# A fused graph-network kernel: two layer-1 steps a turn in the last gate blocks, adjacencies two packs ahead, head rounds with conv1 first

## The chip, the cores and the metric

The kernel runs on one core of one Trainium2 chip. The metric is the device time of the program in microseconds. Before the change it is 2128.19 us, the median of three runs (2126.38 to 2130.4). Engines are named as in the profile: PE (TensorE matmuls) and PEld (its weight loads), DVE (VectorE), ACT (ScalarE), POOL (GpSimd) and SP (SyncE, which here only issues DMAs). Line numbers are those of the kernel before.

## The reference, cut to what matters

Two residual layers over `x` of 128 graphs x 128 nodes x 256 features, all in float32.

```python
# layer 0
h = relu(layernorm(x))
hc = relu(bn1(conv1(h^T)))                    # 1x1 convolution over features
x_conv = relu(bn2(conv2(hc)) + h^T)^T         # 17 taps along the nodes
A = exp(-dist(h @ w_se)) * adj                # 128x128 per graph
x_nmp = A @ relu(h @ w_msg + b_msg)
x = x + GRU([x_conv, x_nmp], h)               # gates r, z, n
# layer 1: only nodes 0 to 24, in 5 groups of 25, 9, 7, 6 and 6 nodes
h = relu(layernorm(x))
for g in range(5):
    a = sym_norm(adj[g] + I)                  # degree^-1/2 on both sides
    fused[nodes of g] += w[g] * relu(a @ (relu(a @ (h_g @ W1[g]) + b1[g]) @ W2[g]) + b2[g])
x = x + fused
```

Rows of nodes 25 and up are final after layer 0 (up to the residual); layer 1 needs layer 0 of its graphs complete.

## The kernel before

A block is four graphs (512 node rows, `BB = 4`), so there are 32 blocks, in two halves of 16. The program has three stages.

**Heads and spectra.** conv2 is done as a product of spectra. Each half runs `heads` (L249): for block i the layer norm (`head_norm`, DVE with a power on POOL, L144 to L151), the transposes to features-first (`head_turn`, PE L201, ACT L202, stored to DRAM at L203), conv1 (`head_conv1`, PE L215, DVE L218, ACT L219) and the block's spectra (`head_spectra`, PE L230, copied into `X` by DVE L236 and ACT L238). The pieces of different blocks are staggered within one round of the loop. Beside the first half the spectra of the taps are made, `weight_spectra` (L165): 8 groups of 4 steps, 32 in all; a step is 16 matmuls into four PSUM banks (L172), emptied by two DVE (L178) and two ACT (L180) copies, and after its fourth step a group of 2,560 KB goes to DRAM (L182). `some_spectra(k)` takes k steps; six are taken ahead of `heads`, and `heads` calls it at its two `between()` places a round. Then `spectral` (L266) multiplies the spectra, 40 frequencies a half, with `v` loaded from DRAM; it begins the next half's heads near its end (`heads_begin`).

**Gates.** For each of 32 blocks `gates` (L530) computes the three GRU gates by a seven-product scheme; each unit has seven products (PE L550), and after each product it calls `between()`, 22 times a block with the one at L588. That is `step` (L845): odd calls advance `beside_gates(i + 1)` (messages, inverse transform, edges and the residual `back(i - 1)` for other blocks), and even calls, and odd ones once that is exhausted, take one step of layer 1. `back` (L608) transposes the first 25 nodes (PE L622, waiting for DVE's L617) and stores them to DRAM as rows `xg`.

**Layer 1.** The graphs are cut into parts of 32, 32, 32, 16, 8 and 8 (`PARTS`). `layer1(k)` (L690) is a generator that starts when all blocks of part k are through; part 4 starts behind block 30, part 5 in the tail. A part's graphs are packed by group into up to 128 rows. For a pack: `pack_load` (L645: `adj`, `hg` from DRAM), `pack_rows` (L655: degree and norm, DVE with a power on POOL L670, and a block-diagonal matrix `bd`, L676 and L679), `pack_adj` (L682: PE transposes `bd`, L685, and DVE scales it into `nt`, L687). Then a step is one pack's first product with `nt` (PE L766, DVE L767), or W1 of half the hidden columns of a group in this chunk (PE L783, ACT/DVE L788/L790), or W2 of one pack (PE L800, ACT L802) with the closing product of the pack before (`last`, PE L729, ACT L732, DVE L738). `prepare(j)` runs these stages ahead: loads of pack j + 5, rows of j + 3, `nt` of j + 1. A part waits 8 empty steps after its first loads. W1 and W2 of a group are loaded into rings of 2 and 3 buffers (L704), and a part's result is stored at L813.

The order on each engine is fixed when the program is built: a list scheduler moves instructions within what the dependences and the rings of buffers allow, and an engine then runs its list in order. DMAs issued on SP run through one such list as well, so a DMA that waits holds up those listed behind it. The tail is written out by hand: finish all but the last generator, run part 4 until it says that all its packs are loaded, start part 5, finish.

Of the kernel before, what the change touches and what calls it, by code (L numbers as in the profile page):

```python
# [66 lines left out]
def gnn_kernel(ctx: ExitStack, tc: tile.TileContext, io, out0: bass.AP, out1: bass.AP):  # L67
# [119 lines left out]
    def head_load(wk, i, queue):  # L187
        xs[i] = wk.tile([P, BB, D], F32, tag="ln", name="ln", bufs=3)
        queue.dma_start(xs[i], x[i * BB:(i + 1) * BB].rearrange("b n d -> n b d"))
# [4 lines left out]
    def head_turn(wk, i):  # L194

        ln = xs.pop(i)
        ht = wk.tile([P, C, T], F32, tag="ht", name="ht", bufs=2)
        for c in range(C):
            ps = bank()
            for b in range(BB):  # L200
                nc.tensor.transpose(ps[:, b * N:(b + 1) * N], ln[:, b, c * P:(c + 1) * P], ident)  # L201
            nc.scalar.activation(ht[:, c, :], ps, AF.Relu)  # L202
        nc.scalar.dma_start(htd[i], ht)  # L203
        hcs[i] = ht
# [44 lines left out]
    def heads(wk, X, h, between):  # L249

        i0, i1 = h * NBH, (h + 1) * NBH
        for i in range(i0, i1 + 1):
            if i + 3 < i1:
                head_load(wk, i + 3, nc.sync)
            if i + 2 < i1:
                head_norm(wk, i + 2)
            if i + 1 < i1:
                head_turn(wk, i + 1)
            between()
            if i < i1:  # L260
                head_conv1(wk, i)
            between()
            if i > i0:
                head_spectra(X, i - 1)
# [60 lines left out]
    with front as es:  # L325
        xp = es.enter_context(tc.tile_pool(name="xp", bufs=1))
        hk = es.enter_context(tc.tile_pool(name="hk", bufs=1))
        X = xp.tile([P, C, NP_, 2, P], F32)
        with ExitStack() as ws:
            wp = ws.enter_context(tc.tile_pool(name="wp", bufs=1))  # L330
            todo = [(c, q) for c in range(C) for q in range(D // WCH)]
            head_load(hk, 0, nc.scalar)
            nc.sync.dma_start(gt, io["gt"])
            taps = [taps_load(wp, *todo[k]) for k in range(2)]
            head_norm(hk, 0)
            spectra = []

            def some_spectra(k=1):
                for _ in range(k):
                    if not spectra and todo:  # L340
                        spectra.append(weight_spectra(wp, *todo.pop(0), taps.pop(0)))
                    if spectra and next(spectra[0], STOP) is STOP:
                        spectra.pop(0)
                        if len(todo) > 1:
                            taps.append(taps_load(wp, *todo[1]))
                        some_spectra()

            some_spectra(3)
            constants()
            heads_begin(hk, 0)  # L350
            some_spectra(3)
            heads(hk, X, 0, some_spectra)
            while spectra or todo:
                some_spectra()
        bp = es.enter_context(tc.tile_pool(name="bp", bufs=1))
        nc.sync.dma_start(wms, io["wms"].rearrange("(c p) o -> p c o", p=P))
        nc.sync.dma_start(bms, row("bms", D + 3))
        nc.sync.dma_start(fw, row("fw", 5))
        nc.sync.dma_start(wih, io["wih"].rearrange("(c p) o -> p c o", p=P))
        nc.sync.dma_start(whh, io["whh"].rearrange("(c p) o -> p c o", p=P))  # L360
        for h in range(NH):
            if h:
                heads(hk, X, h, lambda: None)
            spectral(bp, X, h, lambda: heads_begin(hk, h + 1) if h + 1 < NH else None)
            if h == 0:
                gate_weights()
# [278 lines left out]
    def pack_load(k, g, b0, nb):  # L645
        s = GROUPS[g][0]
        n = nb * s
        adj = l1.tile([P, NN], F32, tag="adj", name="adj", bufs=6)
        r0 = (first_of[k] + b0) * s
        nc.sync.dma_start(adj[:n, :s], io[f"adj{g}"][r0:r0 + n, :])  # L650
        hg = l1.tile([P, D], F32, tag="hg", name="hg", bufs=6)
        nc.sync.dma_start(hg[:n], xg[k][g][b0 * s:b0 * s + n, :])
        return adj, hg

# [35 lines left out]
    def layer1(k):  # L690
# [20 lines left out]

        def prepare(j):

            if 0 <= j + 5 < len(packs):
                loads[j + 5] = pack_load(k, *packs[j + 5])
            if 0 <= j + 3 < len(packs):
                g, _, nb = packs[j + 3]
                rows[j + 3] = pack_rows(g, nb, *loads.pop(j + 3))
            if 0 <= j + 1 < len(packs):
                g, _, nb = packs[j + 1]  # L720
                ready[j + 1] = pack_adj(nb * GROUPS[g][0], *rows.pop(j + 1))

        def last(g, b0, nb, s2, nt):

# [13 lines left out]
                    nc.vector.tensor_add(fv, fv, ov[:, c, :, at:at + rn])  # L738
                at += rn

        for j in (-5, -4):
            prepare(j)
        part_rows(k)
        nc.sync.dma_start(f[:, :, :size, :], xf[k])
        yield
        weights1(2)
        weights2(3)
        for _ in range(8):
            yield
        for j in (-3, -2, -1):  # L750
            prepare(j)
            yield
        ends = {g: n + 1 for n, (g, _, _) in enumerate(packs)}
        j = 0
        for chunk in chunks:
# [3 lines left out]
            for g, b0, nb in chunk:  # L759
                n = nb * GROUPS[g][0]  # L760
                prepare(j)
                hg, nt = ready.pop(j)
                j += 1
                ps = bank()
                for c in range(C):
                    nc.tensor.matmul(ps[:, c * P:c * P + n], hg[:n, c * P:(c + 1) * P], nt[:n, :n], start=True, stop=True)  # L766
                nc.vector.tensor_copy(ax[:, :, at:at + n], ps[:, :C * P].rearrange("p (c m) -> p c m", c=C)[:, :, :n])  # L767
                work.append((g, b0, nb, nt, at))
                segs[g] = (segs[g][0] if g in segs else at, at + n)
                at += n  # L770
                if late:
                    last(*late.pop(0))
                yield j + 5 >= len(packs)
            hh = l1.tile([P, HID // P, 512], F32, tag="hh", name="hh", bufs=1)
            for g, (m0, m1) in segs.items():
                m = m1 - m0
# [64 lines left out]
    for i in range(NBLK):  # L841
        first = beside_gates(i + 1)
        turn = [0]

        def step():  # L845

            turn[0] += 1
            if turn[0] % 2 and next(first, STOP) is not STOP:
                return
            while layer1s and next(layer1s[0], STOP) is STOP:  # L850
                layer1s.pop(0)

        if i + 2 < NBLK:
            load(i + 2)
        xts[i] = wk.tile([P, C, T], F32, tag="xt", name="xt", bufs=2)
        nc.sync.dma_start(xts[i], io["xT"][i])

        def nxt():
            for _ in first:
                pass  # L860
            if i + 1 < NBLK:
                gate_inputs(i + 1)

        gates(i, step, nxt)
        for k in range(len(PARTS)):
            if i * BB == first_of[k + 1]:
                layer1s.append(layer1(k))
# [106 lines left out]
```

## Time and profile before

The span of the profiled execution is 2127.4 us. By stages, from the busy time of each engine in windows:

| stage, us from the start | length | PE busy | DVE busy | PE clock | DMA share |
|---|---|---|---|---|---|
| setup, 0 to 28.9 | 28.9 | 17.9 | 19.9 | 0.84 | 0.93 |
| heads, first half, to 204.0 | 175.1 | 159.3 | 109.6 | 0.90 | 0.70 |
| spectral, first half, to 318.6 | 114.6 | 107.4 | 56.8 | 0.97 | 0.79 |
| heads, second half, to 430.7 | 112.1 | 105.3 | 73.9 | 0.97 | 0.45 |
| spectral, second half, to 535.0 | 104.3 | 103.1 | 50.0 | 1.00 | 0.81 |
| gates with layer 1, to 1949.0 | 1414.0 | 1390.5 | 914.7 | 0.99 | 0.29 |
| blocks 30 (its end) and 31, to 2018.6 | 69.6 | 58.2 | 43.6 | 0.93 | 0.19 |
| rest of part 3, to 2033.4 | 14.8 | 14.7 | 2.6 | 0.85 | 0.75 |
| part 4, to 2076.5 | 43.1 | 36.7 | 18.9 | 0.76 | 0.52 |
| part 5, to 2127.4 | 50.9 | 40.4 | 12.9 | 0.71 | 0.22 |

"PE clock" is the share of full speed that was granted. A matmul in float32 shows up as two records, so 16 records of L215 are 8 instructions. The granted clock matters as much as busy time here: a busy PE at clock 0.7 does 0.7 of the work.

### The profile page before, as it was taken

The page shows a single profiled execution, that of the slowest core. Times are in us where ns is not written, and L with a number is a line of the kernel's source. Part 1 is how long each engine was busy: PE and PEld are TensorE (multiplying, and loading weights), DVE is VectorE, ACT ScalarE, POOL GpSimd, SP SyncE. Part 2 cuts the span into 40 slices and gives each one's busy share as a digit, 9 for nine tenths or more (in the row PEclk, how much of TensorE's full clock was granted, in tenths as well). Part 3 has the DMA queues.
Part 4 walks back from the last instruction along what each step waited for, and adds up shares of the span by engine and source line. Part 5 has one row for each costly group of instructions (what it writes and reads, how often), then busy time and mean ns, then how long its engine had stood idle before and what let it go on. Part 6 is the DMA issues. An engine that isn't in the chain of part 4 may idle for free.

```text
span 2127.4 us, 30421 instructions
## 1 busy us (share of the span) xinstructions
PE 2033.4 (96%) x10725; PEld 1696.2 (80%) x10725; DVE 1302.8 (61%) x3576; ACT 712.9 (34%) x1456; POOL 574.7 (27%) x666
## 2 busy tenths in 40 slices
PE   7888998999899999999999999999999999998988
PEld 6777888988687887877888787788878878886776
DVE  6665456645366676676666567666666766657532
ACT  3333113411233333333333333333333333332322
POOL 3101441144142342432222243222223322222100
PEclk8989999999999999999999999999999999999977
DMA  8665885378622222322233232223323222322152
GB/s 335 251 229 207 283 277 192 130 234 281 190 66 70 73 72 80 95 68 59 79 90 103 79 101 66 60 74 94 99 77 99 64 64 77 98 66 73 55 167 77
DMA packets 209689, 263.34 MB, mean 124 GB/s; under 512 B 60290, under 2 KB 182146, under 8 KB 204802
## 3 DMA queue, kind: packets, MB, share of 16 engines
q1 hardware_dynamic: 201202, 223.12, 34.6%
q10 hardware_dynamic: 8336, 38.28, 4.9%
q8 instruction: 86, 1.41, 0.3%
q14 instruction: 65, 0.53, 0.1%
HBM read 179.30 MB, written 85.72 MB: 125 GB/s over the span
## 4 chain that ended last, share of the span: by engine, by line
PE 83%; DVE 5%; DMA 2%; POOL 1%; issue 1%; SPq 0%; ACT 0%; POOLq 0%; DVEq 0%; ACTq 0%
PE bank L550 35%; PE bank L299 6%; PE bank L800 5%; PE bank L783 5%; PE bank L586 5%; PE bank L456 5%; PE bank L215 3%; PE bank L294 3%; PE bank L441 3%; PE bank L502 3%; PE bank L439 3%; PE bank L230 2%; PE bank L766 1%; PE bank L489 1%; PE bank L729 1%
## 5 line engine op out<-in xcount | busy, mean ns | idle before, releaser
L550 PE MATMUL bank<-t,sw 128*128 128x256 f32 x1024 | 253.6, 380 | 0.0
L563 POOL TENSOR_TENSOR u<-u,m 128x256 f32<-128x256 f32 x96 | 71.7, 747 | 641.5 <-ACT m L561 618.5
L550 PEld LDWEIGHTS bank<-t,sw 128*128 128x128 f32 x1024 | 187.6, 191 | 23.3 <-issue 1.1
L550 PE MATMUL bank<-t,wih 128*128 128x256 f32 x768 | 197.2, 379 | 0.0
L550 PEld LDWEIGHTS bank<-t,wih 128*128 128x128 f32 x768 | 145.5, 190 | 33.8 <-issue 10.0
L291 POOL TENSOR_TENSOR vs<-v 128x512 f32<-128x512 f32 x78 | 101.4, 1319 | 140.3 <-DMA v<-vd 89.1
L783 PE MATMUL bank<-ax,w 128*128 128x192 f32 (+12 forms) x592 | 130.8, 373 | 5.4 <-DMA w<-in_w_dram 3.9
L800 PE MATMUL bank<-w,hh 128*100 128x256 f32 (+8 forms) x552 | 134.6, 389 | 0.0
L215 PE MATMUL bank<-wc,ht 128*128 128x256 f32 x512 | 129.7, 411 | 1.6 <-DVE sp L178 1.6
L456 PE MATMUL bank<-wms,ht 128*128 128x259 f32 x512 | 126.0, 390 | 4.7 <-DMA ht<-htd 4.7
L783 PEld LDWEIGHTS bank<-ax,w 128*128 128x128 f32 x592 | 106.5, 222 | 23.1 <-issue 13.4
L670 POOL TENSOR_TENSOR pw<-pw,mhalf 100x2 f32<-100x2 f32 (+7 forms) x69 | 51.2, 743 | 260.6 <-DVE pw L666 92.7
L215 PEld LDWEIGHTS bank<-wc,ht 128*128 128x128 f32 x512 | 103.9, 208 | 18.1 <-DVE sp L178 1.8
L456 PEld LDWEIGHTS bank<-wms,ht 128*128 128x128 f32 x512 | 99.9, 195 | 21.0 <-issue 5.1
L550 PE MATMUL bank<-xc,wih 128*128 128x256 f32 x384 | 115.8, 383 | 0.0
L550 PE MATMUL bank<-xn,wih 128*128 128x256 f32 x384 | 115.6, 383 | 0.0
L586 PE MATMUL bank<-ht,whh 128*128 128x512 f32 x256 | 115.2, 592 | 0.0
L738 DVE TENSOR_TENSOR f<-f,og 128x48 f32<-128x48 f32 (+7 forms) x192 | 56.4, 326 | 95.7 <-ACT og L732 94.2
L800 PEld LDWEIGHTS bank<-w,hh 128*100 128x100 f32 (+8 forms) x552 | 92.9, 170 | 27.2
L289 DVE SCALAR_TENSOR_TENSOR s<-X 128x256 f32<-128x256 f32 x78 | 51.7, 665 | 90.6 <-PE bank L299 90.3
L149 POOL TENSOR_TENSOR rs<-ve,mhalf 128x4 f32<-128x4 f32 x32 | 32.3, 1010 | 239.1 <-DVE ve L147 239.1
L460 ACT ACTIVATE msg<-msg 128x512 f32<-128x512 f32 x64 | 40.3, 630 | 157.6 <-DVE msg L457 145.3
(173 smaller groups left out, 4457.0 us busy)
## 6 DMA issues: line engine op xcount, KB each, us to landing
v<-vd SPq DMA_DIRECT2D x80, 512.0 KB
w<-in_w_dram SPq DMA_DIRECT2D x60, 512.0 KB
vd<-sp SPq DMA_DIRECT2D x8, 2560.0 KB
yd<-ys ACTq DMA_DIRECT2D x40, 512.0 KB
htd<-ht ACTq DMA_DIRECT2D x32, 512.0 KB
ht<-htd SPq DMA_DIRECT2D x32, 512.0 KB
ym<-yd SPq DMA_DIRECT2D x32, 512.0 KB
xt<-in_xT_dram SPq DMA_DIRECT2D x32, 512.0 KB
```

What stands on the lines that cost most here:

```text
L215: nc.tensor.matmul(pv[:, bb, :], ht[:, c, b * N:(b + 1) * N], wc1[:, c, :], start=c == 0, stop=c == C - 1)
L291: nc.gpsimd.tensor_tensor(vs, vr, vi, op=ALU.add)
L294: nc.tensor.matmul(p1[:, :D], a[:, c], vs[:, c], start=c == 0, stop=c == C - 1)
L299: nc.tensor.matmul(ps[:, k * D:(k + 1) * D], u[:, c], w[:, c], start=c == 0, stop=c == C - 1)
L439: nc.tensor.matmul(ps, yr[:, o * P:(o + 1) * P], idr, start=True, stop=False)
L441: nc.tensor.matmul(ps[:, b * N:(b + 1) * N], ym[:, b, o * P:(o + 1) * P], idm, start=False, stop=b == BB - 1)
L456: nc.tensor.matmul(ps[:, :D + 3], ht[:, c, b * N:(b + 1) * N], wms[:, c, :], start=c == 0, stop=c == C - 1)
L550: nc.tensor.matmul(ps, w, d, start=n == 0, stop=n == len(pairs) - 1)
L563: nc.gpsimd.tensor_tensor(got["u4"], got["u2"], got["m5"], op=ALU.add)
L586: nc.tensor.matmul(ps, whh[:, c, col:col + P], ht[:, c, :], start=c == 0, stop=c == C - 1)
L783: nc.tensor.matmul(pv[:, q - q0, :], w1s[g][:, c, q * P:(q + 1) * P], ax[:, c, m0:m1], start=c == 0, stop=c == C - 1)
L800: nc.tensor.matmul(ps[:n, :D], hh[:, q, at:at + n], w2s[g][:, q, :], start=q == 0, stop=q == HID // P - 1)
```

## The change

Four edits. In `heads` a round's order becomes conv1(i), tap steps, turn(i+1), norm(i+2), tap steps, spectra(i-1), in both halves; and in the first half each `between()` takes two tap steps instead of one, so that the taps are through by block eight. In layer 1 every stage of `prepare` runs one pack further ahead, with a seventh `hg` buffer and one more preparing step. Small parts pause two steps instead of eight. In the gates of the last two blocks a turn that goes to layer 1 takes two steps. The aim is to take tap work early and to carry part 4 under the last gates.

```diff
         for i in range(i0, i1 + 1):
             if i + 3 < i1:
                 head_load(wk, i + 3, nc.sync)
+            if i < i1:
+                head_conv1(wk, i)
+            between()
+            if i + 1 < i1:
+                head_turn(wk, i + 1)
             if i + 2 < i1:
                 head_norm(wk, i + 2)
-            if i + 1 < i1:
-                head_turn(wk, i + 1)
-            between()
-            if i < i1:
-                head_conv1(wk, i)
             between()
...
-            heads(hk, X, 0, some_spectra)
+            heads(hk, X, 0, lambda: some_spectra(2))
...
-        hg = l1.tile([P, D], F32, tag="hg", name="hg", bufs=6)
+        hg = l1.tile([P, D], F32, tag="hg", name="hg", bufs=7)
...
-            if 0 <= j + 5 < len(packs):
-                loads[j + 5] = pack_load(k, *packs[j + 5])
-            if 0 <= j + 3 < len(packs):
-                g, _, nb = packs[j + 3]
-                rows[j + 3] = pack_rows(g, nb, *loads.pop(j + 3))
-            if 0 <= j + 1 < len(packs):
-                g, _, nb = packs[j + 1]
-                ready[j + 1] = pack_adj(nb * GROUPS[g][0], *rows.pop(j + 1))
+            if 0 <= j + 6 < len(packs):
+                loads[j + 6] = pack_load(k, *packs[j + 6])
+            if 0 <= j + 4 < len(packs):
+                g, _, nb = packs[j + 4]
+                rows[j + 4] = pack_rows(g, nb, *loads.pop(j + 4))
+            if 0 <= j + 2 < len(packs):
+                g, _, nb = packs[j + 2]
+                ready[j + 2] = pack_adj(nb * GROUPS[g][0], *rows.pop(j + 2))
...
-        for j in (-5, -4):
+        for j in (-6, -5):
             prepare(j)
...
-        for _ in range(8):
+        for _ in range(8 if size > 8 else 2):
             yield
-        for j in (-3, -2, -1):
+        for j in (-4, -3, -2, -1):
             prepare(j)
             yield
...
-                yield j + 5 >= len(packs)
+                yield j + 6 > len(packs)
...
-            while layer1s and next(layer1s[0], STOP) is STOP:
-                layer1s.pop(0)
+
+            for _ in range(2 if i >= NBLK - 2 else 1):
+                while layer1s and next(layer1s[0], STOP) is STOP:
+                    layer1s.pop(0)
```

The condition `j + 6 > len(packs)` is the old one written otherwise. The hand-written tail is not touched.

## The prediction

> **What bounds the kernel now.** I read the page first: busy time, then the 40 slices, then the chain that ended last.
>
> ```profile
> PE 2033.4 (96%) x10725; PEld 1696.2 (80%) x10725; DVE 1302.8 (61%) x3576; ACT 712.9 (34%) x1456; POOL 574.7 (27%) x666
> ...
> PEclk8989999999999999999999999999999999999977
> ...
> PE 83%; DVE 5%; DMA 2%; POOL 1%; issue 1%; SPq 0%; ACT 0%; POOLq 0%; DVEq 0%; ACTq 0%
> ```
>
> PE carries the chain. No matmul is added or removed, so what can be won is PE idle time (94 us) and time at a low clock (first four slices, last two). So I asked for windows by stage: setup, first heads, layer-1 tail.
>
> ```profile
> 28.90:204.00 175.10, 159.29 (x1424) 135.87 (x1424) 109.62 (x347) 65.83 (x174) 23.18 (x25) 0.90 0.70 253
> ...
> 535.00:1949.00 1414.00, 1390.52 (x6726) 1137.97 (x6725) 914.66 (x2382) 510.68 (x926) 406.87 (x494) 0.99 0.29 83
> 1949.00:2018.60 69.60, 58.16 (x293) 47.29 (x294) 43.56 (x166) 19.43 (x46) 13.70 (x19) 0.93 0.19 50
> 2018.60:2033.40 14.80, 14.71 (x82) 12.79 (x82) 2.55 (x11) 5.29 (x15) 0.00 (x0) 0.85 0.75 208
> 2033.40:2076.50 43.10, 36.72 (x185) 30.54 (x183) 18.87 (x106) 11.96 (x35) 4.17 (x6) 0.76 0.52 156
> 2076.50:2127.40 50.90, 40.41 (x183) 33.62 (x182) 12.93 (x70) 11.36 (x33) 1.38 (x2) 0.71 0.22 71
> ```
>
> Columns: length; busy PE, weight load, DVE, ACT, POOL; clock; DMA share; GB/s. The gates are full at clock 0.99; the heads run at 0.90, and after the last gate 109 us run at 0.71 to 0.85. Parts 4 and 5 of layer 1 take 43.1 and 50.9 us there although they issue the same instructions. Third, the waits of PE, in the gates (560 to 1900) and after:
>
> ```profile
> PE bank L766 <- DVE nt L687: 13.1, 9, 1.7
> ```
>
> ```profile
> PE bank L622 <- DVE deg L663: 7.2, 1, 7.2
> ...
> PE bank L622 <- DVE xl L617: 4.0, 1, 4.0
> ```
>
> In 1,340 us of gates PE waits for one thing only: an adjacency `nt` that is not scaled yet. The other two are block 30's and 31's residual (`back`), which PE must transpose.
>
> **The Trainium skill.** "TensorE: Matmul & The Clock Gate", What's actually happening: the clock is halved after an idle window and full again after about 3.4 us of sustained work. The trace agrees: conv1's 16 records take 3.62 us in steady state and 5.41 us behind a 2 us wait, so a stall costs about as much again. "PSUM — Partial Sum Buffer", PSUM: the matmul accumulator: eight banks; the kernel takes them one by one, and a tap step takes four. "DMA: Bandwidth & Descriptors", Where 436 GB/s comes from: about 358 GB/s of HBM per core. Windows of 10 us in the front read 337 at share 0.97, 357 at 0.99, 414 at 1.01.
>
> **Heads.** Before, a round does norm(i+2), turn(i+1), tap step, conv1(i), tap step, spectra(i-1). From conv1 of block 1 (37.7) to that of block 13 (180.8) twelve rounds take 11.9 us each. Steady state in the second half is 6.5 us at clock 1 (starts: L201 344.83, L215 345.70, L230 349.15, L201 351.33), and a tap step is 1.06 us, so 8.7 us of work, 1.2 us of waits (14.5 us in the stretch) and 2.0 of slow clock. After, four tap steps lie in a round, so 22 of the 32 remain when conv1 of block 1 starts (ten are issued then, nine before): 5.5 rounds, and 9.5 rounds without.
> - Tap rounds. PE 6.5 + 4 x 1.06 = 10.7. A wait: the norm, now between the two pairs of steps, takes DVE about 4.5 us (statistics 1.9, POOL's rs 1.2, L151 1.3), while PE has 3.1 us of work (turn, two steps) until spectra needs a bank that DVE empties behind the norm: 1.4 us. Slow clock 1.9 as now. Together 14.0. Transfers by the page's list: vd 2560, taps 1024, x 512, htd 512 KB = 4.72 MB a round, at 370 GB/s (middle of 337 to 414) 12.8 us, bounds 11.4 and 14.0. So the two limits are close; I take 14.0: 77 us.
> - The rest: 9.5 x 6.5 = 62, plus 3 for x loads that share the SP queue with the first v loads, plus the last spectra 2.2.
> - Start at 38.5 (one step more than 37.7): end 38.5 + 77 + 65 + 2.2 = 182.7 against 204: -21. An x load is issued behind a 2.56 MB store and lands some 10 us later; some rounds will wait for it. I take -18.
>
> The second half's heads are saturated in steady state, so the order of the three pieces costs and brings nothing. Their start waits 6.8 us (L201 <- L218) because a norm blocks DVE until its x load lands; in the changed order that norm still stands ahead of the next L218: nothing, +-2.
>
> **Two packs ahead.** pack_adj moves one step earlier, so `nt` gets a step more (3 to 6 us) against waits of 1.0 to 1.7: of 13.1 I take -12. The earlier loads and rows cost nothing: same instructions, same distances load to row to adjacency, so the ring of 6 `adj`, 3 `bd` and the 7th `hg` suffice; the gates hide them. One more preparing step per part shifts work by a step and costs nothing.
>
> **Blocks 30 and 31, and the tail.** A turn that goes to layer 1 takes two steps there, and the small parts pause 2 steps, not 8. Counted from the generators: before, block 30 gets 13 steps and block 31 gets 21, leaving 9 of part 3, then part 4 (35) and part 5. After, 26 and 42: part 3 is finished and part 4 has 7 steps left.
> - Moved under the gates, at full clock: part 3's rest, L783 16 x 0.213 = 3.4, L800 4 x 1.73 = 6.9, L729 5 x 0.42 = 2.1, so 12.4 (it took 14.8). Part 4 but 7 steps: L685 0.6, L766 2.7, L783 8 x 0.333 + 32 x 0.213 = 9.5, so 12.8 (27.6 now, 2033.4 to 2061). Blocks 30 and 31 grow by 25.2.
> - They lose: the 7.2 us wait of L622 (two L800 and two L729, 4.3 us, now lie ahead of it, and no pack's rows stand in DVE at that point), 1.7 of nt, and 2.2 of slow clock behind them; of 15.2 with the 4.0 at the end, about 5 stays (3.4 of it before the last L622, one L783 group ahead of it instead of another).
> - They gain hazards: two packs or two L783 groups per turn leave a w1 load (3.6 us from issue to landing by the chain) about 4.3 us, an `nt` about 2.2. Not shown before; between 0 and 10, I take 4.5. So L622 of block 31 ends 25.2 - 15.2 + 5 + 4.5 = 19.5 us later.
> - From that L622 (T) to the end it is 108.8 now. After: 7 steps of part 4, 6 x 1.73 + 7 x 0.42 = 13.4 us. Then part 5, which before had all of part 4 (43 us) to load its rows. Now its rows of groups 1 to 4 come late: `while len(layer1s) > 1` does not run, the loop over part 4 finds no step that says all is loaded and runs it out, and only then is part 5 started. On the SP queue its four hg loads stand behind part 4's output store, which waits for part 4's last add (T + 15.5), a copy, the f load and three w2 loads: issued T + 18 to 19.5, at 0.3 to 0.65 each. The w2 loads are 1.5 MB, 4.5 us, ahead of them: the first hg lands about T + 24. Rows 3.2 us, then 1.6 a pack, last transpose, nt, L766: L783 starts at T + 33.5. Bounds 28 (loads overtake) and 38. From L783 to the end as now: 2127.4 - 2085.6 = 41.8, its clock 0.58 included. So T + 75.3: 33.5 less.
> - Sum of the tail: 19.5 - 33.5 = -14.
>
> **Sum.** 2127.4 - 18 - 12 - 14 = 2083.4 of span; the device time is 0.8 above the span here, two in the profiled run: 2085.
>
> **Rivals.**
> 1. Transfers set the tap rounds (17.5 us instead of 14: a DMA share of 0.93 before 28.9 us, under the densest transfers, speaks for it, 0.70 in the heads against): heads end near 202, -2 instead of -18: 2101.
> 2. The tail brings nothing: hazards 10 and part 5 at T + 38 (+10), or worse: 2098. For it: DVE is 71% busy (37.4 of 53 us) from 1915 to 1968.
> 3. Both go better: transfers at 400 GB/s and no x waits (-25), no hazards and hg loads early (-25): 2066.
> 4. Slower: tap rounds at 18.7 (store, x load and norm one behind another: 38.5 + 103 + 65 + 2.2 = 209, +5), part 5's rows 15 us later still and hazards 15 (+12), and the nt waits come back as waits for `bd` (0): 2145. Against it: inside the gates of before PE never waits for `bd`, and the share of DMA there is 0.29.
>
> **Chances.** Forecast 0.50, rival 1 0.20, rival 2 0.12, rival 3 0.12, slower 0.06. The range 2062 to 2112 holds the first and the third rival's centre and the larger part of the bounds above (hazards 0 to 10, hg 28 to 38, transfers 11.4 to 14). Faster 0.91, within 0.2% 0.03, slower 0.06.
>
> **What would show it.** Heads: conv1 starts 14 us apart while L172 lasts, then 6.5; last L230 of the first half near 186. Gates: no wait of L766 for nt. Blocks 30 and 31: L622's wait under 2 us, then about 3.5. Tail: from the last L622 about 75 us, with 12 to 16 us in which PE waits for rows (L685 <- bd, behind a DMA of hg). Wrong would be: tap rounds over 16 us, an x load named ahead of L144 in every round; L783 in block 31 waiting for w several times; hg landing before T + 18.

## The result, and the profile after

The changed kernel takes 2099.28 us (median of four runs, 2098.28 to 2102.21) against 2128.95 us for the kernel before: a ratio of 0.9864, 95% interval 0.9847 to 0.9881. The forecast was 2085: the direction was right and the time lies in the range, but the gain is 29.7 us where 43 were forecast. So two questions were put to the chip: where the missing 13 us went, and whether they can be had.

The page of the changed kernel, with the lines that answer those shown of before:

```profile
PE 2006.7 (96%) x10725; PEld 1675.0 (80%) x10725; DVE 1301.2 (62%) x3576; ACT 713.7 (34%) x1456; POOL 574.9 (27%) x666
...
PEclk9899999999999999999999999999999999999986
...
PE 82%; DVE 7%; DMA 6%; POOL 2%; issue 1%; SPq 1%; ACT 0%; POOLq 0%; DVEq 0%; ACTq 0%
```

PE idle fell only from 94 to 90 us; its busy time fell by 27, with the same matmuls, for the most part since they ran less often at the low clock (granted clock of the execution 0.976 for 0.967). The chain now goes over DMA for 6% (2% before), about half of it one kind of transfer, the x loads of the heads (2.8% of the span). Busy time by stage (columns: length; busy PE, weight load, DVE, ACT, POOL; clock; DMA share; GB/s), for the first heads, the gates up to block 29's residual, blocks 30 and 31 up to the last transpose L622 (T), part 4's last seven steps, the wait for part 5's rows, and part 5:

```profile
28.90:193.40 164.50, 148.85 (x1416) 131.12 (x1416) 110.95 (x355) 68.48 (x178) 24.41 (x25) 0.90 0.74 273
546.50:1912.80 1366.30, 1359.30 (x6604) 1113.50 (x6603) 900.13 (x2346) 499.90 (x911) 393.10 (x475) 1.00 0.29 82
1912.80:2018.16 105.36, 96.02 (x549) 80.51 (x547) 66.69 (x270) 34.07 (x83) 22.93 (x30) 0.98 0.32 95
2018.16:2034.05 15.89, 15.89 (x74) 10.79 (x75) 3.64 (x17) 6.23 (x18) 0.71 (x1) 0.89 0.48 132
2034.05:2058.77 24.72, 7.07 (x31) 5.92 (x30) 9.65 (x55) 2.50 (x7) 2.87 (x4) 0.53 0.30 91
2058.77:2096.90 38.13, 31.31 (x153) 25.89 (x152) 6.54 (x29) 9.71 (x28) 0.00 (x0) 0.77 0.24 75
```

The waits of PE in the gates, and then from T to the end:

```profile
PE bank L783 <- DVE ax L767: 5.0, 3, 1.7
PE bank L729 <- ACT s L802: 2.0, 3, 0.7
```

```profile
PE bank L685 <- DVE bd L679: 17.7, 4, 15.4
PE bank L622 <- DVE xl L617: 2.7, 1, 2.7
PE bank L783 <- DMA w<-in_w_dram: 2.3, 2, 2.0
```

The wait for `nt` is gone, 7 us of other waits have come; in the tail one wait of 15.4 us stands where PE has nothing to do until part 5's rows are there. The clearest account is that of a few marks, the same matmul in each trace (the last column is the best kernel of this study, e12_place below):

| mark, us from the start | before | after | gain so far | best |
|---|---|---|---|---|
| first product of the spectral stage (L284) | 207.53 | 194.06 | 13.5 | 178.07 |
| first gate product (L550) | 558.69 | 546.51 | 12.2 | |
| block 0's transpose (L622) | 621.27 | 609.09 | 12.2 | 589.99 |
| block 28's transpose | 1888.64 | 1863.97 | 24.7 | 1847.39 |
| last transpose, T | 2018.14 | 2018.16 | 0.0 | 2001.61 |
| end | 2127.4 | 2096.9 | 30.5 | 2067.3 |

Heads bring 12.2, the gates 12.5, blocks 30 and 31 take 24.7 more (work moved into them), the tail 30.5 less.

### The profile page after: what moved, and what is told of

The parts are those of the page before. It is cut to its first block, busy times and chain, and to the rows that moved or that the text cites. A ratio compares the mean times of both kernels' runs of the same rounds, so it can differ in the third digit from the quotient of the medians.

```text
span 2096.9 us, 30386 instructions
## 1 busy us (share of the span) xinstructions
PE 2006.7 (96%) x10725; PEld 1675.0 (80%) x10725; DVE 1301.2 (62%) x3576; ACT 713.7 (34%) x1456; POOL 574.9 (27%) x666
## 4 chain that ended last, share of the span: by engine, by line
PE 82%; DVE 7%; DMA 6%; POOL 2%; issue 1%; SPq 1%; ACT 0%; POOLq 0%; DVEq 0%; ACTq 0%
PE bank L550 34%; PE bank L800 6%; PE bank L299 5%; PE bank L586 5%; PE bank L456 5%; PE bank L783 5%; PE bank L215 4%; DMA ln<-in_x_dram 3%; PE bank L502 3%; PE bank L230 3%; PE bank L294 3%; PE bank L441 2%; PE bank L439 2%; DMA v<-vd 2%; PE bank L729 1%; PE bank L489 1%
## 5 line engine op out<-in xcount | busy, mean ns | idle before, releaser
L550 PE MATMUL bank<-t,sw 128*128 128x256 f32 x1024 | 254.7, 382 | 0.0
L550 PEld LDWEIGHTS bank<-t,sw 128*128 128x128 f32 x1024 | 188.4, 191 | 24.6 <-issue 1.7
L550 PE MATMUL bank<-t,wih 128*128 128x256 f32 x768 | 197.2, 379 | 0.0
L550 PEld LDWEIGHTS bank<-t,wih 128*128 128x128 f32 x768 | 145.5, 190 | 34.1 <-issue 10.0
L215 PE MATMUL bank<-wc,ht 128*128 128x256 f32 x512 | 128.1, 406 | 13.0 <-ACT ht L202 10.3
L800 PE MATMUL bank<-w,hh 128*100 128x256 f32 (+8 forms) x552 | 133.4, 386 | 0.0
L783 PE MATMUL bank<-ax,w 128*128 128x192 f32 (+12 forms) x592 | 120.9, 351 | 7.4 <-DVE ax L767 5.0
L215 PEld LDWEIGHTS bank<-wc,ht 128*128 128x128 f32 x512 | 102.7, 206 | 31.0 <-ACT ht L202 13.0
L783 PEld LDWEIGHTS bank<-ax,w 128*128 128x128 f32 x592 | 96.7, 201 | 24.0 <-issue 9.9
L586 PE MATMUL bank<-ht,whh 128*128 128x512 f32 x256 | 115.2, 593 | 0.0
L550 PE MATMUL bank<-xc,wih 128*128 128x256 f32 x384 | 114.4, 380 | 0.0
L550 PE MATMUL bank<-xn,wih 128*128 128x256 f32 x384 | 114.2, 379 | 0.0
L800 PEld LDWEIGHTS bank<-w,hh 128*100 128x100 f32 (+8 forms) x552 | 92.2, 169 | 26.7
L441 PEld LDWEIGHTS bank<-idm,ym 128*128 128x128 f32 x512 | 67.2, 192 | 30.6 <-issue 29.9
L230 PE MATMUL bank<-fd,h 128*128 128x160 f32 x512 | 82.5, 317 | 9.0 <-DVE sp L178 9.0
```

Of the source, the lines that this page charges most:

```text
L215: nc.tensor.matmul(pv[:, bb, :], ht[:, c, b * N:(b + 1) * N], wc1[:, c, :], start=c == 0, stop=c == C - 1)
L230: nc.tensor.matmul(ps[:, bb * 2 * LW:(bb + 1) * 2 * LW], h1[:, 2 * h + bb, c * P:(c + 1) * P], fd, start=True, stop=True)
L441: nc.tensor.matmul(ps[:, b * N:(b + 1) * N], ym[:, b, o * P:(o + 1) * P], idm, start=False, stop=b == BB - 1)
L550: nc.tensor.matmul(ps, w, d, start=n == 0, stop=n == len(pairs) - 1)
L586: nc.tensor.matmul(ps, whh[:, c, col:col + P], ht[:, c, :], start=c == 0, stop=c == C - 1)
L783: nc.tensor.matmul(pv[:, q - q0, :], w1s[g][:, c, q * P:(q + 1) * P], ax[:, c, m0:m1], start=c == 0, stop=c == C - 1)
```

## The experiments

All ratios are to the kernel before, with 95% intervals. Profiles of kernels whose front is the same differ there by some us (block 0's transpose at 609.1 in the changed kernel, 614.0 in e4_tail, 611.0 in e6_tail2), so in what follows a stage is measured between its own marks.

### The three edits one at a time

**e1_heads**: before, with only the edits to the head rounds.

```diff
+            if i < i1:
+                head_conv1(wk, i)
+            between()
             if i + 1 < i1:
                 head_turn(wk, i + 1)
...
-            heads(hk, X, 0, some_spectra)
+            heads(hk, X, 0, lambda: some_spectra(2))
```

> The kernel before with only the edits to the head rounds (conv1 first, two tap steps at each place). Theory A, the parts are separate: the traces of before and after stand 12.2 us apart at the first gate matmul (558.7 and 546.5), and nothing of that is given back later, so this kernel takes 12 us less than before, 2116 to 2118. Theory B, an earlier start of the gates is partly given back (a wait that ends on a transfer and not on the heads): 4 to 8 us less, 2120 to 2125. In both, tap rounds of about 16 us from conv1 to conv1, and one wait of PE per tap round on a bank that VectorE has not emptied (L230 behind L178), 1.4 to 2.8 us.

Measured: 2116.19 us, ratio 0.9947 (0.9928 to 0.9967), 12.3 us less. Theory A: block 0's transpose comes at 609.13 (changed kernel 609.09, before 621.27), and nothing of it is given back later. That the two marks agree so closely is chance, since the same front scatters by some us.

**e2_ahead**: before, with only `prepare` a pack further ahead, `hg` in seven buffers and the four preparing steps.

```diff
-            if 0 <= j + 1 < len(packs):
-                g, _, nb = packs[j + 1]
-                ready[j + 1] = pack_adj(nb * GROUPS[g][0], *rows.pop(j + 1))
+            if 0 <= j + 2 < len(packs):
+                g, _, nb = packs[j + 2]
+                ready[j + 2] = pack_adj(nb * GROUPS[g][0], *rows.pop(j + 2))
```

> The kernel before with only the adjacencies prepared two packs ahead. Theory A: the waits of L766 for nt (13.1 us in the gates) go, and waits of L783 for ax and of L729 for s of 7 us come, as in the changed kernel; with the slow clock behind each, 10 us less than before up to block 30, and nothing in the tail: 2117 to 2120. Theory B: the new waits come from the shift of the chunks by one turn and cost as much as they save: 2124 to 2129. If the new waits are absent here, they belong to the shorter pauses or the two steps, not to this edit.

Measured: 2125.00, ratio 0.9981 (0.9970 to 0.9993): 3.5 us less. The time lies in theory B's range, but not for B's reason. Its waits of PE in the gates:

```profile
PE bank L783 <- DVE ax L767: 6.0, 3, 2.5
PE bank L729 <- ACT s L802: 1.4, 2, 0.7
```

So the new waits belong to this edit. From block 0's to block 28's transpose it takes 1257.6 us (before 1267.4, changed kernel 1254.9), 9.8 less, as theory A has it. But its tail is 115.0 us from T to the end instead of 109.3: with all of parts 4 and 5 behind T, PE waits there 6.2 us for w1 loads (3.9 before).

**e3_two**: before, with only the two steps a turn and the pause of two steps.

```diff
-        for _ in range(8):
+        for _ in range(8 if size > 8 else 2):
...
+            for _ in range(2 if i >= NBLK - 2 else 1):
```

> The kernel before with only the two steps a turn in the last two blocks and the shorter pauses. Theory A, separate: blocks 30 and 31 grow by 22 us, the tail after the last transpose falls by 30: 8 us less, 2119 to 2122. Theory B, two packs in one turn need the adjacencies two ahead: PE waits for nt at every second L766 in blocks 30 and 31, 1 to 2 us each with the slow clock behind it, 6 to 10 us in all: 2126 to 2131.

Measured: 2125.48, ratio 0.9984 (0.9973 to 0.9996): 3.0 us less, between the theories. From block 28's transpose to T it takes 157.7 us where the changed kernel takes 154.2 and before 129.5; from T to the end 77.2 (before 109.3). The nt waits of theory B are there but small:

```profile
PE bank L766 <- DVE nt L687: 2.2, 5, 1.0
```

Together the three single edits give 18.8 us and the whole change 29.7. The traces show two places where a single edit pays: without two steps a turn the adjacency edit pays 5.7 us in the tail, and without the adjacency edit the two steps pay 3.5 us more in blocks 30 and 31. But how much more the whole is worth than its parts is not settled: the four intervals combine to some 6.5 us, and by the profiled spans the single gains are 15.8, 5.7 and 5.4 us, 26.9 together, against 30.5.

### The wait in the tail

The SyncE queue of the changed kernel behind T (columns: start, length, line, DMA):

```profile
2019.10 1.11 SPq L625 DMA_DIRECT2D xg<-xr  x1
2023.72 0.37 SPq L704 DMA_DIRECT2D w<-in_w_dram  x1
2024.15 0.43 SPq L652 DMA_DIRECT2D hg<-xg  x1
...
2026.30 3.52 SPq L642 DMA_DIRECT2D xg<-xg  x5
2035.52 0.60 SPq L813 DMA_DIRECT2D out_dram<-f  x1
2036.16 0.62 SPq L642 DMA_DIRECT2D xg<-xg  x1
2036.83 0.43 SPq L744 DMA_DIRECT2D f<-xf  x1
2037.37 1.48 SPq L704 DMA_DIRECT2D w<-in_w_dram  x3
2038.91 2.67 SPq L652 DMA_DIRECT2D hg<-xg  x4
```

The queue stands from 2029.8 to 2035.5, because part 4's output store L813 waits for part 4's last sum, and the four row loads are behind it. The first lands at 2046.85 (L667 begins), T + 28.7.

**e4_tail**:

```diff
     back(NBLK - 1)
-    while len(layer1s) > 1:
-        step()
-    for loaded_all in layer1s[0]:
-        if loaded_all:
-            break
     layer1s.append(layer1(len(PARTS) - 1))
     next(layer1s[-1])          # and layer1 issues all row loads of this part here
```

> The changed kernel, with part 5 of layer 1 begun directly behind the last block's residual, its six row loads issued with it, and part 4's last steps behind that in the program. Theory A, the 15.4 us wait of PE in the tail is the row loads standing behind part 4's output store, the f load and three w2 loads on the SyncE queue: the loads are issued at T+12 to 15 instead of T+21 (T: the last transpose L622), land at T+18, and the first L783 of part 5 starts at T+29 to 31 instead of T+40.6: 9 to 12 us less than the changed kernel, 2087 to 2090. Theory B, the copies of the rows from DRAM to DRAM and the chain of the rows on VectorE set the wait, and the order of the queue only part of it: 2 to 5 us less, 2094 to 2097, with L685 still waiting 10 us for bd.

Measured: 2097.82, ratio 0.9853 (0.9832 to 0.9875). From T to the end 71.4 us, 7.3 less than the changed kernel, so between the theories. The median is only 1.5 us below the changed kernel's, which is within the intervals; in this profile the front stands 4.9 us later, so the gain is read from the stage alone. The row loads came at T + 12.1 and had landed by T + 14.0 (2040.02), as theory A has it, but they pushed another load back, as the timeline of PE shows:

```profile
2045.34 3.65 PE L806 MATMUL bank<-w,hh 128*48 128x256 f32 x8 [6.48 <-DMA w<-in_w_dram]
```

That is part 4's last group (L800, six lines further down here), waiting for its w2, whose load now stood behind the rows.

**e6_tail2**: the same, with part 4's next three steps, and so its w2 loads, traced between the row copies and the row loads.

```diff
     layer1s.append(layer1(len(PARTS) - 1))
     next(layer1s[-1])          # adjacencies, copies of rows
+    for _ in range(3):
+        next(layer1s[0])       # part 4, with its w2 loads
+    next(layer1s[-1])          # row loads
```

> The kernel of e4_tail, but the four late row loads come behind the w2 loads of part 4 in the program, so that part 4's last group no longer waits for its weights. e4_tail took 71.5 us from the last L622 to the end (the changed kernel 78.7) with 6.5 us of wait of L800 for w2 in it. Theory A, the queue's order alone decides: that wait falls to 0 to 3 us, the first L783 of part 5 starts at T+27 to 31: 66 to 69 us from T, 2087 to 2091. Theory B, the rows' chain of VectorE and GpSimd (2 us a pack) takes its place: 70 to 72 us from T, 2091 to 2095.

Measured: 2097.04, ratio 0.9838 (0.9815 to 0.9862); from T to the end 72.5, no better than e4_tail. The w2 wait fell to 2.99, and a wait of 2.89 for ScalarE came instead, which stood 5.0 us at the relu of a row pack (L674) that VectorE had not normalised yet, with part 4's L802 behind it. First L783 of part 5: T + 32.2. This is theory B's mechanism, the rows' chain, a little above its range in the time: each wait taken off the queue uncovers the next.

### The tap rounds

A tap round is a round of the head loop that holds tap steps. From conv1 of block 1 to that of block 6 the changed kernel has five full tap rounds, 77.86 us, 15.6 each (16.3 and 16.2 in the profiles of e4_tail and e6_tail2, whose front is the same). One of them, on PE and then on VectorE:

```profile
68.83 3.96 PE L215 MATMUL bank<-wc,ht 128*128 128x256 f32 x16
72.72 2.03 PE L172 MATMUL bank<-gt,w 17*128 17x80 f32 x64
74.68 1.09 PE L201 MATMUL bank<-ident,ln 128*128 128x128 f32 x8
...
78.45 0.81 PE L230 MATMUL bank<-fd,h 128*128 128x160 f32 x4
80.66 3.57 PE L230 MATMUL bank<-fd,h 128*128 128x160 f32 x12 [1.40 <-DVE sp L178]
84.02 4.89 PE L215 MATMUL bank<-wc,ht 128*128 128x256 f32 x16
```

```profile
73.91 0.89 DVE L178 COPY sp<-bank 128x320 f32<-128x320 f32 x2 [0.39 <-PE bank L172]
75.01 0.75 DVE L144 BATCH_NORM_STATS2 st<-ln 128x6 f32<-128x256 f32 x2 [0.21 <-DMA ln<-in_x_dram]
...
76.47 0.87 DVE L178 COPY sp<-bank 128x320 f32<-128x320 f32 x2
...
78.82 1.38 DVE L151 TENSOR_SCALAR ln<-ln,mv,rs 128x256 f32<-128x256 f32 x4 [1.12 <-POOL rs L149]
80.12 1.68 DVE L178 COPY sp<-bank 128x320 f32<-128x320 f32 x4
```

L230 waits for a bank whose copy stands behind the norm. The wait is 1.40 us, but the twelve L230 behind it take 3.57 us at half clock (sixteen take 2.34 at full clock) and conv1 4.89 instead of 3.62: 3.1 us more. "TensorE: Matmul & The Clock Gate" of the Trainium skill (What's actually happening) has the clock decided per free-running window of 3413 ns. The trace agrees: its stretches of half clock are 3.413 us long or a multiple of that. But that section asks for an idle window, and here a wait of 1.40 us among small matmuls was enough. In the changed kernel's gates, waits of 1.65 us were not followed by half clock (1.00 there); before, two of the six waits of 1.7 us for `nt` were (clock 0.83 from 1477 to 1482 us, 0.84 from 1851 to 1858), the other four not (1.00).

**e5_norm**: the norm ahead of conv1 in the round.

```diff
+            if i + 2 < i1:
+                head_norm(wk, i + 2)
             if i < i1:
                 head_conv1(wk, i)
             between()
             if i + 1 < i1:
                 head_turn(wk, i + 1)
-            if i + 2 < i1:
-                head_norm(wk, i + 2)
             between()
```

> The changed kernel with one line moved: the norm of block i+2 stands ahead of conv1 of block i, not between the two pairs of tap steps. Theory A, the tap rounds take 16.2 us because VectorE does the norm (4.3 us) while PE waits for the banks behind it, and because each such wait of 1.4 to 2.8 us is followed by 3 us of slow clock: with the norm under conv1, where VectorE is idle for 3.4 us, the wait of L230 for L178 (9.0 us in five rounds) goes and the rounds take 13 to 14 us, set by the transfers: 10 to 15 us less than the changed kernel, 2085 to 2090. Theory B, the wait only moves (a tap step or L230 then waits for h or sp behind the late L218, or the norm waits for its x load): rounds of 15 to 17 us, 2096 to 2102.

Measured: 2100.30, ratio 0.9859 (0.9834 to 0.9883), tap rounds of 16.2 us, as in other profiles of the unmoved front. The time is theory B's, but the run does not test A: the scheduler left the norm where it was in VectorE's order, between the L178 of a round. What it placed it by showed only later.

**e7_order**: the changed kernel with one tap step at each place.

> The changed kernel with one tap step at each place instead of two: the order conv1, tap, turn, norm, tap, spectra alone. Theory A, what a tap round loses (2.0 us of waits, 3.4 of slow clock) is lost per round, so that half as many tap steps a round lose it twice as often: the front's 12 us are given back, 2108 to 2113. Theory B, it is lost per tap step (banks emptied too slowly for four steps in a row): 2097 to 2102, and conv1 to conv1 11 us over 11 rounds.

Measured: 2111.80, ratio 0.9906 (0.9875 to 0.9938), and the first gate product at 556.51, 10.0 us later than in the changed kernel: theory A. Its rounds from conv1 of block 1 to that of block 13 take 12.2 us each (before 11.9): the new order by itself makes no round shorter. Fewer tap rounds do.

**e8_best**: e5_norm and e6_tail2 in one.

> Both repairs at once, norm ahead of conv1 and the tail of e6_tail2. The two lie 1,800 us apart, so they should add: if theory A of both holds 2074 to 2081, if only the tail's 2087 to 2091, if neither 2095 to 2100.

Measured: 2096.10, ratio 0.9840 (0.9817 to 0.9862), which lies in the range that was given for no gain from either repair. Its trace has tap rounds of 16.3 us, so nothing from the front; from T to the end it has 72.5 us, the 6 us of e6_tail2, of which the medians show 1 to 3, within the intervals.

**e9_act**: the taps behind the norm are emptied by ScalarE alone.

```diff
-                if r % 2:
+                if r % 2 and not acts:        # acts: set around the second between()
                     nc.vector.tensor_copy(dst, s)
```

> The changed kernel, where the tap steps behind the norm are emptied by ScalarE alone (8 copies of 0.43 us a round, ScalarE idles some 7 us of a tap round) instead of four by each engine. In e5_norm the norm stayed where it was in VectorE's order, between the L178 of a round, so that run did not test what it was meant to; this one takes the copies away from behind the norm. Theory A, L230 waits for banks whose copies stand behind the norm in VectorE: the wait (9.0 us in five rounds) falls to under 3 us, its slow clock (3.4 us a round) to about 1, rounds of 13 to 14 us from conv1 to conv1: 10 to 15 us less, 2085 to 2090. Theory B, PE waits as long for ScalarE (8 copies take 3.0 us, PE's two tap steps 2.0) or for the x loads: rounds of 15 to 16.5 us, 2095 to 2101.

Measured: 2101.45, ratio 0.9873 (0.9848 to 0.9899). The waits of L230 for L178 went, as A had it, and rounds without a wait took 11.8 and 13.0 us. But two of the five took 17, and all together 74.6 (14.9 each). A long one, on VectorE and on PE:

```profile
89.98 0.75 DVE L144 BATCH_NORM_STATS2 st<-ln 128x6 f32<-128x256 f32 x2 [3.44 <-DMA ln<-in_x_dram]
```

```profile
91.96 2.40 PE L172 MATMUL bank<-gt,w 17*128 17x80 f32 x32 [3.44 <-DVE sp L178]
```

VectorE stands at a norm whose x load has not landed, and what PE needs stands behind it. The x load had been issued at 77.96, 12 us earlier.

**e10_copies**: e9_act with the tail of e6_tail2, and four of the seven row copies of part 5 issued by ScalarE.

```diff
         for g, (s, runs) in enumerate(GROUPS[1:], 1):
+            queue = nc.scalar if k == len(PARTS) - 1 and g > 2 else nc.sync
...
-                nc.sync.dma_start(dst[:, at:at + rn], src[:, r0:r0 + rn])
+                queue.dma_start(dst[:, at:at + rn], src[:, r0:r0 + rn])
```

> e9_act and the tail of e6_tail2 in one, and the copies of the rows of groups 3 and 4 issued by ScalarE's queue instead of SyncE's, so that the w2 load of part 4's last group (2.99 us of wait in e6_tail2) and the row loads come 2 us earlier. From the last L622 to the end e6_tail2 took 72.5 us. Theory A, the SyncE queue's order and length still set the tail: 66 to 69 us, and with e9_act's gain 2075 to 2083 (2087 to 2093 if that has none). Theory B, the rows' chain (hg lands, VectorE, GpSimd, VectorE, transpose, nt) sets it: 71 to 73 us.

Measured: 2092.43, ratio 0.9826 (0.9801 to 0.9851). From T to the end 70.4 us in the profile (e9_act 78.0), between the theories; the w2 wait 2.2 us.

**e11_xqueue**: e10_copies, and x comes on ScalarE's queue.

```diff
             if i + 3 < i1:
-                head_load(wk, i + 3, nc.sync)
+                head_load(wk, i + 3, nc.scalar if h == 0 else nc.sync)
```

> e10_copies, and in the first half's heads the x loads go to ScalarE's queue instead of SyncE's, where each is issued 0.4 us behind a 2.56 MB store of tap spectra and lands 12 to 16 us later. In e9_act the bank waits were gone, but every second tap round still took 17 us (51.9 to 69.0, 80.9 to 97.9), because the norm waited for its x (12.5 us in four waits of L144). Theory A, the place behind the store sets those rounds: x lands within 6 us, the waits of L144 go and all tap rounds take 12 to 13.5 us, so that the first product of the spectral stage (194.1 in the changed kernel, 190.5 in e9_act) starts at 177 to 183: 8 to 13 us less than e10_copies (2092), 2079 to 2084. Theory B, the transfers' volume sets them (4.7 MB a round): x lands no earlier, or the stores and tap loads land later in its place, rounds of 14 to 16 us, 2089 to 2095.

Measured: 2144.91, ratio 1.0096 (1.0069 to 1.0122), slower than before. Neither theory. VectorE in the five tap rounds, which take 24.1 us each:

```profile
DVE st L144 <- DMA ln<-in_x_dram: 71.2, 5, 14.7
```

x issued at 60.10 is first used at 73.37, when VectorE has stood at it for 14.65 us: it lands no sooner for not standing behind the store in its queue. "DMA: Bandwidth & Descriptors" (Queues, rings and completion order) says why that can be: SyncE's and ScalarE's queues are rings on the same 16 DMA engines, which take turns between them packet by packet. The trace agrees: 13.3 us for 512 KB beside the store, a tap load and an htd store, 4.7 MB in all. From 65 to 69 us, with the store (q1, SyncE) and x (q10, ScalarE) under way, as many packets of one pass as of the other (columns: packets, MB, share of the 16 engines):

```profile
q1 hardware_dynamic: 77, 1.58, 92.7%
q10 hardware_dynamic: 77, 0.08, 5.7%
```

The store's packets are some 20 KB and those of x 1 KB, so equal turns leave x a twentieth of the bytes. And the norm now stands ahead of L218 in VectorE's order, so that conv1's banks wait as well. This names the cause that had been missed: a norm does not run where it is written, but where the scheduler puts it. (That the scheduler goes by its own model of when x has landed is inferred from these orders; the runs show the orders.) In the changed kernel the norm of x(6), written in the round of block 4, runs in that of block 3 (x issued at 60.95, norm from 75.01). It stands until x has landed; the last copies of the taps stand behind it; the store waits for them, and the next x load is issued behind the store:

```profile
60.95 0.39 SPq L189 DMA_DIRECT2D ln<-in_x_dram  x1
...
77.41 0.33 SPq L182 DMA_DIRECT2D vd<-sp  x1
77.83 0.48 SPq L189 DMA_DIRECT2D ln<-in_x_dram  x1
```

A loop of x load, norm and store sets the round: from one x issue to the next it is 16.9 us here, and 13.8 to 16.9 in these rounds. The chain of the changed kernel in these rounds (36.9 to 114.8 us) says it in one line:

```profile
by line: DMA ln<-in_x_dram 52.7%; PE bank L230 9.2%; PE bank L215 8.6%; PE bank L172 8.3%; DVE ln L151 7.0%; DVE st L144 5.3%; POOL rs L149 3.9%; DVE sp L178 3.6%; PE bank L201 2.6%; issue 1.6%; DVE mv L145 1.3%; DVE ve L147 0.7%; POOLq L14
```

**e12_place**: e10_copies, with an edge of order (no wait) that keeps the norm in its own round.

```diff
             if i + 2 < i1:
-                head_norm(wk, i + 2)
+                with tc.issue_after(behind[0].ins) if h == 0 else ExitStack():
+                    head_norm(wk, i + 2)      # behind: the last L178 or L218 traced
```

> e10_copies, and the norm of the first half's heads is tied behind the last VectorE instruction traced ahead of it (the last L178 of the first pair of tap steps), an edge of order alone. In the changed kernel the norm of x(6) runs in the round of block 3 (x issued 60.95, norm from 75.01), a round ahead of where it is written, since the scheduler's model holds x landed; on the chip x lands 12 to 16 us after its issue, VectorE stands at L144, and what stands behind it (bank copies, then the next store and x load) goes round with it. e11_xqueue, with x on another queue, lands x no sooner (issued 60.10, norm at 74) and has rounds of 24 us since the norm was hoisted further. Theory A, this loop over the x load's latency sets the tap rounds: with the norm in its written round its x was issued 25 us earlier, the waits of L144 go, and tap rounds take 12.5 to 13.5 us (4.72 MB at 350 to 370 GB/s): the spectral stage starts at 177 to 184 instead of 194, 8 to 14 us less than e10_copies (2092), 2079 to 2085. Theory B, the transfers' volume and the bank copies set them: rounds of 14.5 to 16 us, 2089 to 2095.

Measured: **2074.45 us, ratio 0.9741 (0.9718 to 0.9765)**: 18.0 us less than e10_copies, 24.8 less than the changed kernel, and better than both. Theory A. No norm waits for x in its rounds, and they take 13.6 us (33.01 to 101.01). In the profiles the spectral stage starts 16.1 us earlier than in e10_copies (178.07 for 194.14): 3.0 before conv1 of block 1, 7.2 in the five rounds, 6.4 in the round behind them. The five rounds of the changed kernel, of e10_copies and of this one:

```profile
36.90:114.76 77.86, 67.83 (x845) 59.22 (x842) 48.65 (x141) 31.14 (x82) 8.95 (x10) 0.85 0.86 337
```

```profile
36.03:111.18 75.15, 69.67 (x844) 62.52 (x841) 41.14 (x126) 37.97 (x105) 8.94 (x10) 0.82 0.88 337
```

```profile
33.01:101.01 68.00, 59.30 (x841) 53.88 (x841) 37.80 (x117) 38.22 (x107) 8.75 (x10) 0.90 1.00 389
```

Much the same volume (25.3 to 26.5 MB) now keeps all DMA engines busy. What PE and ScalarE wait for there is the transfers themselves, the tap loads and the stores:

```profile
PE bank L232 <- ACT sp L180: 7.0, 3, 4.4
PE bank L172 <- DMA w<-in_w2t_dram: 1.7, 1, 1.7
```

```profile
ACT sp L180 <- DMA vd<-sp: 9.2, 3, 5.1
```

## Why the prediction was right, and where it was 13 us too good

By its own steps, each with forecast and measurement (the sum: -44 of span forecast, -30.5 measured).

1. **Heads, -18 forecast, -12.2 measured.** The count of rounds and of tap steps held, and so did the start (conv1 of block 1 at 36.9; 38.5 forecast). The failing step is "A wait: the norm, now between the two pairs of steps ... 1.4 us. Slow clock 1.9 as now. Together 14.0". A full tap round takes 15.6: its work 10.7, waits 2.0, and 2.9 for the rest. Two things stood wrong in it. The 1.9 was carried over from rounds whose waits were smaller, and it was no reading of the clock but what was left of a round: the granted clock, 0.90 from 37.7 to 180.8 before and 0.85 in the five rounds after, allows at most 1.2 and 2.3 us a round. And the norm was taken to run where it is written; it runs a round earlier, for an x that has not landed. "An x load ... lands some 10 us later; some rounds will wait for it" was on record and priced at 3 us; it lands after 12 to 15 us and, by way of the norm, the copies and the store, sets the round. e12_place shows it by its removal: 13.6 us, near the 14.0 of the forecast, though there it is the transfers that set them. The rest of the half took 3.7 us more than forecast (67.6 us from conv1 of block 7). By luck 2.8 came back at the spectral stage's first product, which waited 3.5 us before and 0.7 after; 1.3 of it was lost again by the first gate product. Second heads at +-2: their x wait stayed (L215 behind L202, 6.1 us, for L201's 6.8).
2. **Rival 1, transfers set the tap rounds at 17.5.** Not in the changed kernel: share 0.86, 337 GB/s. With the loop gone they do, at 13.6 us: 5.3 MB a round at 389 GB/s. The forecast's 12.8 had the rate low (370). Its volume of 4.72 MB is not refuted: only 22.5 of the 26.5 MB were issued within the five rounds, the rest was under way before (a store, a tap load, an x load, 768 KB of weights).
3. **Two packs ahead, -12 forecast, -12.5 measured** to block 28, of which some 1.7 is a layer-1 step that now falls behind that mark (PE has 9 records fewer in the stretch, 6081 for 6090; a step has 8). The nt waits went to nothing, as forecast; but that the sum is so near is luck. PE's waits in the stretch fell by 6.8 us only (13.1 to 6.3), and its busy time fell by 5.7: the 1.7 of that step, and slow clock behind two of the nt waits (up to 3.4 us), which the forecast had not counted. "One more preparing step per part shifts work by a step and costs nothing" was wrong: the shift takes a chunk's first L783 away from behind the long L586, and it waits for `ax`, behind the `nt` and the rows in VectorE's list: 5.0 and 2.0 us, in e2_ahead as well.
4. **Blocks 30 and 31, +19.5 forecast, +24.7 measured.** The step counts were exact: part 3 finished, seven steps of part 4 left. Waits went from 12.9 to 10.0 us, near the forecast (-3.4 net). PE's busy time rose by 27.6 where 23 was forecast: 1.7 is the step at the mark, and most of the slow clock that was to go stayed, since L685 now waits for `bd` (4.4 us in four waits) where two packs go in one turn; behind the last of these six L550 take 2.93 us instead of 1.46. About 1 us is not accounted for. L622 of block 30 waits 0.3 us (under 2 forecast), the last 2.7 (3.5 forecast).
5. **Tail, -33.5 forecast, -30.5 measured.** The mechanism was called by name and is there: row loads behind the output store, 15.4 us of wait (12 to 16 forecast). Sizes: part 4's seven steps 15.9 us (13.4; the first sixteen L800 records took 5.30 instead of 3.46); row loads issued at T + 20.8 (18 to 19.5), first landing T + 28.7 (24); rows to L783 11.9 us at clock 0.50 (9.5), so L783 at T + 40.6, outside the bounds 28 to 38; then 38.1 to the end (41.8).

So the direction was right, and so were the mechanisms of the gates and the tail that the forecast named; it missed the new waits for `ax` and the placing of the norm. The heads' term, in which the latter lies, is the largest of the error (5.8 of 13.5 us), blocks 30 and 31 make 5.2, the tail 3.0, the gates -0.5. The sign of being wrong that was put on record for the heads, tap rounds over 16 us with an x load named ahead of L144 in every round, was nearly met: 15.6 us (16.3 and 16.2 in e4_tail and e6_tail2), and x named in three of the five rounds. The rival "the tail brings nothing" (2098) has the measured time, but not for its reason.

What stays open: whether the edge of order does as much without e9_act's copies on ScalarE, which e12_place keeps; how much of e12_place's tap rounds could still be saved now that transfers bound them, and what of the tail's 66 to 72 us in the repaired kernels is clock; the same tail took 70.4 us in e10_copies' profile and 65.7 in e12_place's, by L783 and L800 at half or at full clock.

## What to carry to other kernels

Ask of every instruction not where it is written but where it stands in its engine's list, and what the scheduler believed when it put it there: a norm placed a round early, for a load that was late, cost 18 us, and an edge of order alone took that back. A wait that goes round a loop (load, norm, bank copy, store, next load) shows as a few short waits of PE and as one large share in the chain; read the chain when the waits look too small for the time. And when a wait is taken off a queue, look for what was waiting behind it: e4_tail, e6_tail2 and e10_copies each uncovered the next.

## What the runs showed of the hardware that was not expected

- A 512 KB load took 12 to 15 us beside a 2.56 MB store on the same queue (changed kernel), and 13.3 us on the other queue (e11_xqueue): the second queue did not make it faster. There the two queues passed equal numbers of packets (77 and 77 in 4 us), which were 20 KB on one side and 1 KB on the other.
- The DMA engines kept up 389 GB/s at a share of 1.00 for 68 us (e12_place), 26.5 MB of loads and stores mixed; that is more than the 358 GB/s that the prediction quotes.
- Half clock comes in stretches of 3.413 us and multiples. A wait of 1.40 us in a tap round cost 3.1 us more at half clock in the changed kernel; in e12_place one of 1.38 us was followed by full speed (L230's sixteen records in 2.44 us) and one of 1.23 us by half speed (4.12 us); and in the gates before, the same wait of 1.7 us was followed by half clock two times in six. What a short wait costs is not settled by its length.
